# Second attention of a two-layer hybrid block: diagonal blocks from TensorE transposes, and the seam comparison in front of the last additions

## The chip, the cores and the metric

The kernel runs on one core of one Trainium2 chip. The metric is device time in microseconds of one execution. Everything is fp32. TensorE multiplies (a result lands in PSUM, in tiles of 128 partitions), ScalarE applies functions such as the exponential, VectorE and GpSimd do elementwise work, and queues move data between SBUF and HBM. The engines run side by side and wait for each other on semaphores.

## The reference

The input x has 8 images of 128 channels and 48 x 48 = 2304 positions. Two layers follow each other. The first is a causal attention over the positions, with a group norm in front. The second has two parts: a softmax attention without weights over layer-normed tokens, and then a batch-normed recurrence over layer-normed tokens.

```python
# layer 0
x = x + causal_attention(group_norm(x), Wq, bq, Wk, bk, Wv, bv)
# layer 1
t = to_tokens(x)                              # (8, 2304, 128)
h = layernorm(t)
attn = softmax(einsum('bnd,bmd->bnm', h, h))  # the second attention
t = t + einsum('bnm,bmd->bnd', attn, h)
# recurrence over the 2304 tokens
Wx = batchnorm(layernorm(t) @ W.T)
y_t = sigmoid(Wx_t + y_{t-1} @ V.T)
t = t + y
```

What matters here: in the second attention queries, keys and values are the same normed tokens h. The matrix of scores h h^T is symmetric, and so is its exponential. Each row is then divided by its own sum.

## The kernel before

**Blocks and chunks.** The 2304 tokens of an image are 18 blocks of 128 (`NB`), or 6 chunks of 384 (`NQ` chunks of `QC` columns, `QB` = 3 blocks each). For a chunk j of queries the second attention needs, for each block m of keys, p = exp(h_m h_j^T), a tile of 128 keys x 384 queries, and sums up h_m^T p in PSUM. The symmetry is already used between chunks: for blocks m behind the chunk (m's chunk over j) p is computed ("direct"), stored transposed through HBM, and read again as g when the other chunk comes ("turned"). Within a chunk's own 3 x 3 blocks it is not used: all three own tiles are computed in full.

**One step of the stream.** Each step has two halves. `begin` multiplies the scores and takes the exponential, with the row sums as a by-product. `product` multiplies p into the result, three steps later (`LAG = 3`). TensorE's stream is thus: score of step n, product of step n - 3, score of step n + 1, and so on; in "turned" steps only the product.

```python
class Full:
    def begin(self, j, what, first):
        b = self.b
        if first and j == 0:
            self.rows = small2.tile([P, NB, NQ], F32, tag="rows", name=f"rows_{b}")
        ...                                                     # cut: other chains, prefetch
        if what[0] == "turned":
            ...
            return self.loaded[i, j][:, :, g, :, :].rearrange("p a m r -> p m a r"), 0.0
        m = what[1]
        xh = x_hat[b][1]
        s = psum_s(f"s1_{b}_{j}_{m}")
        nc.tensor.matmul(s[:, :QC], xh[:, ts(m, P)], xh[:, ts(j, QC)], start=True, stop=True)   # L1212
        p = pp.tile([P, QC], F32, tag="p", name=f"p1_{b}_{j}_{m}")
        nc.scalar.activation(p, s[:, :QC], AF.Exp, bias=shift,
                             accum_out=self.rows[:, m, j : j + 1])                              # L1214
        return p, st.then(st.spend(QC * US), [("ACT", 0.58)])

    def product(self, j, what, o, p, ready, first, last):
        xhT = x_hat[self.b][0]
        if what[0] == "turned":
            ...
            nc.tensor.matmul(out_ap, xhT[:, QB * i + g, :], p, start=first, stop=last)          # L1222
        else:
            nc.tensor.matmul(o[:, :QC], xhT[:, what[1], :], p, start=first, stop=last)          # L1226
            if what[1] // QB > j:
                self.turned(j, what[1], p, ready)               # VectorE transposes p, to be stored
```

`st` is a bookkeeping of expected times that decides at build time where chains of smaller work are put into the stream; it issues nothing itself. `psum_s` has 4 buffers of one PSUM bank each, the pool of p has 6. The order of instructions is fixed by the program (`manual_schedule`). A chunk's own blocks come last in its list of direct steps, or first where j = 0. Chunk j = 0 shares its first steps with the end of the causal attention, and in the last chunk the steps of the next image's causal attention are interleaved.

**End of a chunk.** `after` turns the sums back to token-major order and adds the residual. `far` chooses between two ways for that, and is off in this attention (`FULL_FAR = False`). `sums` adds up `rows[:, 3j : 3j + 3, : j + 1]`.

**The recurrence.** The 2304 tokens are cut into 96 segments of 24 (`LS`), in three groups of 32 (`G`). All segments run side by side, each with a warm-up of 12 steps, so there are 36 steps for each group. In front of it stands a row of products whose result is not used (`idle`):

```python
idle(pw[:, 2 * P :], 14)                      # L1392: each an fp32 128x128 product
...
for t in range(-WARM, LS):
    for g in range(G):
        if s == 0 and t + TZ < LS:
            zs[g].append(inputs(g, t + TZ))   # VectorE, L1488: z = wx * a + c into PSUM
        nc.tensor.matmul(z[:, s], vT_f, prev[g], start=False, stop=True)    # L1539
        nc.scalar.activation(to, z[:, s], AF.Sigmoid)                       # L1541
        if s == TZ - 1:
            l0 = t + 1 - TZ
            if 0 <= l0 and (g or l0 >= LM):   # LM = 20
                if t < LS - 1:
                    add_residual(g, l0, y[g][:, so + 1 - TZ : so + 1])
            elif ...:                         # group 0 below LM: added by an accumulating DMA
        if t == LS - 1:
            seams(g)                          # last state of a segment against the next one's warm state

nc.vector.tensor_reduce(off, dm, AX.X, ALU.max)
nc.vector.tensor_scalar(off, off, STATE_TOL, None, ALU.is_gt)
for g in range(G):
    add_residual(g, LS - TZ, y[g][:, TO[g] - TZ :])
    if g:
        continue
    ...                                       # the flag: should the general path be run instead?
```

`add_residual` (L1521, L1522) adds on GpSimd for l0 < 20 and on VectorE for l0 = 20 and 22, and stores the result. Its VectorE buffers (`rlast`) are 3. `seams` is three VectorE operations for a group, two for the last (L1512 to L1515).

Of the kernel before, what the change touches and what calls it, by code (L numbers as in the profile page):

```python
# [14 lines left out]
F32 = mybir.dt.float32  # L15
AF = mybir.ActivationFunctionType
ALU = mybir.AluOpType
AX = mybir.AxisListType
# [586 lines left out]
def fast_path(ctx: ExitStack, tc: tile.TileContext, x, pe, w_ffn, out, x_tok, w_qkv, w_pos, v_t, gamma_beta, flag):  # L605
    nc = tc.nc
    B, C, H, W = x.shape
    N = H * W
    P = 128
    assert C == P and N % P == 0  # L610
    NB = N // P
    CH = 512
    QC = 384
    NQ = N // QC
    QB = QC // P
    SCALE = 1.0 / math.sqrt(P)
    US = 4 / 2400.0
# [7 lines left out]
    LS = N // SEGS  # L625
# [5 lines left out]
    LM = LS - 4  # L631
# [9 lines left out]
    ident = cpool.tile([P, P], F32, tag="ident", name="ident")  # L641
# [20 lines left out]
    with ExitStack() as actx:  # L662
# [11 lines left out]
        small2 = actx.enter_context(tc.tile_pool(name="small2", bufs=2))  # L674
# [4 lines left out]
        def psum_s(name):  # L679
            return ps_s.tile([P, CH], F32, tag="s", name=name)  # L680

        def psum_t(name):
            return ps_t.tile([P, CH], F32, tag="t", name=name)
# [43 lines left out]
        shift = apool.tile([P, 1], F32, tag="shift", name="shift")  # L727
# [45 lines left out]
        CAUSAL_FAR, FULL_FAR = True, False  # L773
        st = Stream()
# [341 lines left out]
        class Full:  # L1116
# [72 lines left out]
            def begin(self, j, what, first):  # L1189
                b = self.b  # L1190
                if first and j == 0:
                    self.rows = small2.tile([P, NB, NQ], F32, tag="rows", name=f"rows_{b}")
                if j == 0:
                    st.finish(normed_chunks[b, what[1] // QB])
                if first and b + 1 < B:
                    if j == 1:
                        norm_chain[b + 1] = st.add(group_norm(b + 1))
                    if j == NQ - 2:
                        st.finish(norm_chain[b + 1])
                        project(b + 1, 0)  # L1200
                self.prefetch()
                if what[0] == "turned":
                    i, g = what[1:]
                    while (i, j) not in self.loaded:
                        while self.pairs[len(self.loaded)] not in self.stored:
                            self.store()
                        self.load()
                    return self.loaded[i, j][:, :, g, :, :].rearrange("p a m r -> p m a r"), 0.0
                m = what[1]
                xh = x_hat[b][1]  # L1210
                s = psum_s(f"s1_{b}_{j}_{m}")
                nc.tensor.matmul(s[:, :QC], xh[:, ts(m, P)], xh[:, ts(j, QC)], start=True, stop=True)  # L1212
                p = pp.tile([P, QC], F32, tag="p", name=f"p1_{b}_{j}_{m}")
                nc.scalar.activation(p, s[:, :QC], AF.Exp, bias=shift, accum_out=self.rows[:, m, j : j + 1])  # L1214
                return p, st.then(st.spend(QC * US), [("ACT", 0.58)])

            def product(self, j, what, o, p, ready, first, last):
                xhT = x_hat[self.b][0]
# [13 lines left out]
            def after(self, j, o):  # L1232
                b, rows, tsum = self.b, self.rows, self.tsum
                cols = ts(j, QC)
                c = {}
                last = b == B - 1 and j >= NQ - 2
                far = FULL_FAR and not last
                if far:
                    ot = turn_result(o, f"f_{b}_{j}", c, True)
                    at = st.then(st.now, [("DVE", 0.57)])  # L1240
                    through = token_major(c, ot, f"f_{b}_{j}", "tof", 4)
                else:
                    o_sb = chunk_tile("o", f"of_{b}_{j}", c, 2)
                    nc.scalar.copy(o_sb, o[:, :QC])
                    at = st.then(st.now, [("ACT", 0.5)])
# [3 lines left out]
                def sums():  # L1249

                    dn = small2.tile([P, QB], F32, tag="dn", name=f"dn_{b}_{j}")
                    nc.vector.tensor_reduce(dn, rows[:, QB * j : QB * (j + 1), : j + 1], AX.X, ALU.add)
                    n = NQ - 1 - j
                    if n:
                        tp = psum_t(f"ts_{b}_{j}")
                        k = n * R * QB
                        nc.tensor.matmul(
                            tp[:, :k], same.rearrange("p a c -> p (a c)"), tsum[j][:, :n, :].rearrange("p n k -> p (n k)"),
                            start=True, stop=True,
                        )  # L1260
                        own = small2.tile([P, NQ - 1, R, QB], F32, tag="own", name=f"own_{b}_{j}")
                        nc.vector.tensor_mul(
                            own[:, :n].rearrange("p n a g -> p (n a g)"), tp[:, :k], mine[:, :n].rearrange("p n a g -> p (n a g)")
                        )
                        more = small2.tile([P, QB], F32, tag="more", name=f"more_{b}_{j}")
                        nc.vector.tensor_reduce(more, own[:, :n].rearrange("p n a g -> p g (n a)"), AX.X, ALU.add)
                        nc.vector.tensor_add(dn, dn, more)
                    ri = small.tile([P, QB], F32, tag="ri", name=f"ri_{b}_{j}")
                    nc.vector.reciprocal(ri, dn)
                    c["ri"] = ri  # L1270
# [100 lines left out]
                else:  # L1371
# [7 lines left out]
                c["chain"] = self.before["chain"] = st.add([  # L1379
                    *through,  # L1380
                    (sums, 0.15, [("DVE", 0.8)]),
                    (residual, 0.0 if far else 0.35, [("DVE", 3.2)]),
                    (rooted, 0.0, [("POOL", 0.9)]),
# [5 lines left out]
        def idle(tp, n):  # L1389

            for _ in range(n):
                nc.tensor.matmul(tp[:, :P], ident, ident, start=True, stop=True)  # L1392
# [26 lines left out]
        ready, o = {}, {}  # L1419
        for n in range(len(stream) + LAG):  # L1420
            if n < len(stream):
                part, j, what, first, last = stream[n]
                ready[n] = part.begin(j, what, first)
            if n >= LAG:
                part, j, what, first, last = stream[n - LAG]
# [12 lines left out]
    G = SEG_GROUPS  # L1438
    TZ = 2
    TO = [4] + [2] * (G - 1)  # L1440
    assert LS * SEGS == N and WARM % TZ == 0 and LS % TO[0] == 0 and SG * B * TZ == CH
    with ExitStack() as rctx:
        rc = rctx.enter_context(tc.tile_pool(name="rconst", bufs=1))
        rst = [rctx.enter_context(tc.tile_pool(name=f"rst{g}", bufs=4 if g == 0 else 6)) for g in range(G)]
        rres = rctx.enter_context(tc.tile_pool(name="rres", bufs=6))
        rlast = rctx.enter_context(tc.tile_pool(name="rlast", bufs=3))
        ps_z = [rctx.enter_context(tc.tile_pool(name=f"ps_z{g}", bufs=2, space=PSUM)) for g in range(G)]
        ps_w = rctx.enter_context(tc.tile_pool(name="ps_w", bufs=1, space=PSUM))

# [12 lines left out]
        pw = ps_w.tile([P, CH], F32, tag="w", name="pw")  # L1462
# [3 lines left out]
        for t in range(-WARM, -WARM + 2 * TZ, TZ):  # L1466
            for g in range(G):
                z = ps_z[g].tile([P, TZ, B, SG], F32, tag="z", name=f"z_{g}_{t}")
                nc.tensor.matmul(z.rearrange("p t b s -> p (t b s)"), zero[:, :P], zero, start=True, stop=True)
                banks[g].append(z)  # L1470
        idle(pw[:, 2 * P :], 14)

        mv = rc.tile([P, 2], F32, tag="bn_mv", name="bn_mv")
        nc.vector.bn_aggr(mv, stats)
# [23 lines left out]
        prev, warm, y = [], [], [None] * G  # L1498
# [10 lines left out]
        def seams(g):  # L1509
# [4 lines left out]
                nc.vector.tensor_sub(d[:, g, :, SG - 1 :], prev[g][:, :, SG - 1 :], warm[g + 1][:, :, 0:1])  # L1514
            nc.vector.tensor_reduce(dm[:, g : g + 1], d[:, g, :, :n], AX.XY, ALU.max, apply_absolute_value=True)  # L1515

        def add_residual(g, l0, yt):
            engine, pool = (nc.gpsimd, rres) if l0 < LM else (nc.vector, rlast)
            r = pool.tile([P, TZ, B, SG], F32, tag="r", name=f"r_{g}_{l0}")
            t2 = t2s[g].rearrange("p b (s l) -> p l b s", l=LS)[:, l0 : l0 + TZ] if g else t2l[:, l0 - LM : l0 - LM + TZ]  # L1520
            engine.tensor_add(r, yt, t2)  # L1521
            nc.sync.dma_start(out[g, :, l0 : l0 + TZ], r)  # L1522
# [7 lines left out]
        for t in range(-WARM, LS):  # L1530
            s = t % TZ
            for g in range(G):
                if s == 0 and t + TZ < LS:
                    zs[g].append(inputs(g, t + TZ))
                so = t % TO[g]
                if so == 0:
                    y[g] = rst[g].tile([P, TO[g], B, SG], F32, tag="y", name=f"y_{g}_{t}")
                z = zs[g][0]
                nc.tensor.matmul(z[:, s], vT_f, prev[g], start=False, stop=True, skip_group_check=True)  # L1539
                to = warm[g] if t == -1 else y[g][:, so]  # L1540
                nc.scalar.activation(to, z[:, s], AF.Sigmoid)  # L1541
                prev[g] = to
                if t == -1 and g == 0:
                    nc.vector.memset(warm[0][:, :, 0:1], 0.0)
                if s == TZ - 1:
                    zs[g].popleft()

                    l0 = t + 1 - TZ
                    if 0 <= l0 and (g or l0 >= LM):
                        if t < LS - 1:  # L1550
                            add_residual(g, l0, y[g][:, so + 1 - TZ : so + 1])
                    elif l0 >= 0 and so == TO[0] - 1:
                        nc.gpsimd.dma_start(out[0, :, t + 1 - TO[0] : t + 1], y[0], accum_op=ALU.add)
                if t == LS - 1:
                    seams(g)

        off = rc.tile([P, 1], F32, tag="off", name="off")
        nc.vector.tensor_reduce(off, dm, AX.X, ALU.max)
        nc.vector.tensor_scalar(off, off, STATE_TOL, None, ALU.is_gt)
        for g in range(G):  # L1560
            add_residual(g, LS - TZ, y[g][:, TO[g] - TZ :])
            if g:
                continue
            nc.tensor.matmul(pw[0:1, P : P + 1], off, ones[:, 0:1], start=True, stop=True)
            nc.vector.tensor_scalar(flag, pw[0:1, P : P + 1], fl[:, 1:2], 0.5, ALU.add, ALU.is_gt)
# [56 lines left out]
```

## Time and profile before

| What | Value |
|---|---|
| Time, median of 3 runs (lowest to highest) | 1782.08 us (1781.37 to 1783.71) |
| Span of the profiled execution | 1780.2 us |
| Mean granted TensorE clock | 0.991 |
| VectorE, ScalarE, GpSimd busy | 74%, 41%, 12% |
| Chain: scores of the second attention (L1212) | 18% |
| Chain: its direct products (L1226) | 18% |
| Chain: its turned products (L1222) | 12% |
| Chain: first attention, scores and products (L1011, L1022) | 17% and 17% |
| Chain: recurrence products (L1539) | 2% |

How to read it: the profile lists each instruction with its engine and line. A group's row gives the busy time, the mean duration of one, and the engine's idle time just before them with what ended it. The chain is followed back from the last instruction to what released it each time, so its shares say which engine's work sets the end. TensorE's products are pipelined: a record lasts longer than the step from one record to the next, and the step is what a product costs in a row. An fp32 product is two records, a transpose is one.

### The profile page before, as it was taken

How to read it: one execution, taken by the hardware profiler on the slowest of the kernel's cores; microseconds unless marked ns; L12 is line 12 of the kernel's file. 1: busy time of each engine (PE TensorE's matmuls, PEld its weight loads, DVE VectorE, ACT ScalarE, POOL GpSimd, SP SyncE). 2: the span in 40 equal slices, each digit the busy share in tenths (PEclk: the TensorE clock that was granted, in tenths of full speed). 3: DMA queues.
4: the chain of work that ended last, by engine and by line, in shares of the span. 5: the costliest groups of instructions: out<-in, count | busy, mean ns of one | idle time of the engine just before them, and what ended most of it. 6: DMA issues, size and time to landing. Idle time of an engine off the chain costs nothing.

```text
span 1780.2 us, 22179 instructions
## 1 busy us (share of the span) xinstructions
PE 1743.5 (98%) x6242; PEld 1093.8 (61%) x6243; DVE 1312.9 (74%) x3361; ACT 735.2 (41%) x1812; POOL 204.9 (12%) x305
## 2 busy tenths in 40 slices
PE   8999999999999999999999999999999999999995
PEld 5666566665666566665666656665666656665574
DVE  4868668866878668786688668786687866876477
ACT  2344424543345423443245433454234442454354
POOL 1110011000110001100110001100011001100026
PEclk8999999999999999999999999999999999999998
DMA  4405662257424584057722574235830576125857
GB/s 142 135 23 191 181 196 90 88 179 196 119 93 133 173 214 125 23 191 191 187 86 89 181 194 121 94 134 164 222 124 23 191 185 179 47 91 180 207 174 200
DMA packets 205576, 256.10 MB, mean 144 GB/s; under 512 B 89889, under 2 KB 175042, under 8 KB 205444
## 3 DMA queue, kind: packets, MB, share of 16 engines
q1 hardware_dynamic: 204492, 251.57, 48.3%
q0 software_dynamic: 720, 2.62, 1.0%
q8 instruction: 52, 0.85, 0.2%
q14 instruction: 80, 0.66, 0.1%
q10 hardware_dynamic: 232, 0.40, 0.1%
HBM read 150.24 MB, written 104.27 MB: 143 GB/s over the span
## 4 chain that ended last, share of the span: by engine, by line
PE 96%; DMA 1%; DVE 1%; issue 0%; ACT 0%; SPq 0%; POOL 0%; ACTq 0%; DVEq 0%; POOLq 0%
PE s L1212 18%; PE o L1226 18%; PE s L1011 17%; PE o L1022 17%; PE o L1222 12%; PE pj L872 4%; PE pj L875 2%; PE z L1539 2%; PE wx L1319 2%; PE tb L932 1%; PE of_t L932 1%; DVE r L1521 0%; PE pb L830 0%; DMA g<-e 0%; DMA x<-in_x_dram 0%
## 5 line engine op out<-in xcount | busy, mean ns | idle before, releaser
L1214 ACT ACTIVATE p<-s,shift 128x384 f32<-128x384 f32 x504 | 292.9, 581 | 486.8 <-PE s L1212 471.5
L1013 ACT ACTIVATE p<-s 128x384 f32<-128x384 f32 (+2 forms) x504 | 232.2, 461 | 440.3 <-PE s L1011 389.4
L1212 PE MATMUL s<-xh 128*128 128x384 f32 x1008 | 410.4, 489 | 0.0
L1226 PE MATMUL o<-p,xhT 128*128 128x384 f32 x1008 | 403.9, 487 | 4.4 <-ACT p L1214 4.4
L1011 PE MATMUL s<-q,k 128*128 128x384 f32 (+2 forms) x1008 | 382.4, 461 | 0.1
L1022 PE MATMUL o<-p,vT 128*128 128x384 f32 (+2 forms) x1008 | 377.8, 457 | 0.0
L1222 PE MATMUL o<-g,xhT 128*128 128x384 f32 x720 | 281.3, 488 | 0.8 <-DMA g<-e 0.8
L1226 PEld LDWEIGHTS o<-p,xhT 128*128 128x128 f32 x1008 | 189.0, 190 | 132.3 <-ACT p L1214 8.7
L1022 PEld LDWEIGHTS o<-p,vT 128*128 128x128 f32 x1008 | 189.0, 191 | 115.0 <-issue 1.1
L1212 PEld LDWEIGHTS s<-xh 128*128 128x128 f32 x1008 | 186.1, 190 | 115.0
L1011 PEld LDWEIGHTS s<-q,k 128*128 128x128 f32 x1008 | 182.8, 191 | 97.2 <-issue 0.6
L1037 DVE TENSOR_TENSOR acc<-acc,p 128x384 f32<-128x384 f32 (+2 forms) x408 | 209.0, 512 | 33.7 <-POOL p L1016 9.1
L1175 DVE STREAM_TRANSPOSE t<-p 128x384 f32<-128x384 f32 x360 | 187.3, 550 | 37.3 <-ACT p L1214 36.1
L1222 PEld LDWEIGHTS o<-g,xhT 128*128 128x128 f32 x720 | 133.2, 190 | 83.2 <-issue 2.2
L1183 DVE TENSOR_REDUCE tsum<-t 128x12 f32<-128x1152 f32 x120 | 162.4, 1353 | 4.2
L877 DVE TENSOR_TENSOR z<-pj,pb 128x384 f32<-128x384 f32 x144 | 78.9, 548 | 110.0 <-PE pj L872 92.0
L1016 POOL TENSOR_TENSOR p<-p,triu 128x128 f32<-128x128 f32 x144 | 72.8, 507 | 607.9 <-ACT p L1013 514.2
L1292 POOL TENSOR_TENSOR roots<-ve_f,mhalf 128x3 f32<-128x3 f32 x48 | 41.1, 856 | 521.0 <-DVE ve_f L916 521.0
L1214 ACT ACTIVATION_READ_ACCUMULATOR p<-s,shift 128x1 f32 x504 | 97.2, 193 | 0.0
L872 PE MATMUL pj<-xn,wT 128*128 128x384 f32 x192 | 79.8, 501 | 1.4 <-DVE xn L865 1.4
L922 POOL TENSOR_TENSOR rs_c<-ve_c,mhalf 128x3 f32<-128x3 f32 x48 | 45.2, 941 | 216.2 <-DVE ve_c L916 213.6
L1320 DVE TENSOR_TENSOR scale<-wx,scale 128x384 f32<-128x384 f32 x46 | 25.4, 552 | 56.3 <-PE wx L1319 56.3
(263 smaller groups left out, 1471.8 us busy)
## 6 DMA issues: line engine op xcount, KB each, us to landing
e<-t SPq DMA_DIRECT2D x120, 576.0 KB
g<-e SPq DMA_DIRECT2D x480, 144.0 KB
pb<-posb_d SPq DMA_DIRECT2D x46, 576.0 KB
t1t<-in_x_tok_dram SPq DMA_DIRECT2D x48, 192.0 KB
t_d<-tt SPq DMA_DIRECT2D x184, 48.0 KB
t2x<-t_d SPq DMA_DIRECT2D x46, 192.0 KB
scale<-rs SPq DMA_DIRECT2D x46, 192.0 KB
x<-in_x_dram SPq DMA_DIRECT2D x14, 576.0 KB
```

What stands on the lines that cost most here:

```text
L872: nc.tensor.matmul(ps[:, :QC], wT[:, j, :], xn, start=True, stop=True)
L877: nc.vector.tensor_add(z, ps[:, :QC], c["pb"][:, j, :])
L1011: nc.tensor.matmul(s[:, off:QC], keys[b][:, ts(m, P)], queries[b, j][:, off:], start=True, stop=True)
L1013: nc.scalar.activation(p[:, off:], s[:, off:QC], AF.Exp, scale=SCALE)
L1022: nc.tensor.matmul(o[:, off:QC], vals[b][:, ts(m, P)], p[:, off:], start=first, stop=last)
L1037: nc.vector.tensor_add(a[:, off:], a[:, off:], p[:, off:])
L1175: nc.vector.transpose(t[:, :, :, g, :].rearrange("p b j r -> p j b r"), p.rearrange("p (j b r) -> p j b r", j=QB, b=R))
L1183: nc.vector.tensor_reduce(self.tsum[j][:, n - j - 1, :], t.rearrange("p b j m r -> p (b j) (m r)"), AX.X, ALU.add)
L1212: nc.tensor.matmul(s[:, :QC], xh[:, ts(m, P)], xh[:, ts(j, QC)], start=True, stop=True)
L1214: nc.scalar.activation(p, s[:, :QC], AF.Exp, bias=shift, accum_out=self.rows[:, m, j : j + 1])
L1222: nc.tensor.matmul(out_ap, xhT[:, QB * i + g, :], p, start=first, stop=last)
L1226: nc.tensor.matmul(o[:, :QC], xhT[:, what[1], :], p, start=first, stop=last)
```

## The change

The change has two parts, and some smaller adjustments.

*First part.* Within a chunk's own 3 x 3 blocks of exp(scores), block (n, i) is the transpose of block (i, n). So for own block n only the columns from n on are multiplied and exponentiated. The i < n columns are taken from the older tiles of the same chunk by TensorE transposes, written into the free columns of the same score tile s, and copied from there into p by ScalarE, which sums their rows as well. This is meant to take work off TensorE: three blocks of scores in nine are replaced by three transposes. `rows` gets one more column for the copies' sums, set to zero beforehand.

*Second part.* At the end of the recurrence the additions for l0 = 20 are no longer made inside the loop. All six VectorE additions come after the loop, and so the seams are compared in front of them and the flag is known earlier. `rlast` gets a fourth buffer.

*Smaller ones.* The idle products in front of the recurrence go from 14 to 8. The condition in `far` is narrower (it stays off in either case).

```diff
                 if first and j == 0:
-                    self.rows = small2.tile([P, NB, NQ], F32, tag="rows", name=f"rows_{b}")
+                    self.rows = small2.tile([P, NB, NQ + 1], F32, tag="rows", name=f"rows_{b}")
+                    nc.gpsimd.memset(self.rows[:, :, 0:1], 0.0)
...
                 s = psum_s(f"s1_{b}_{j}_{m}")
-                nc.tensor.matmul(s[:, :QC], xh[:, ts(m, P)], xh[:, ts(j, QC)], start=True, stop=True)
+                n = m - QB * j if m // QB == j else 0
+                off = n * P
+                nc.tensor.matmul(s[:, off:QC], xh[:, ts(m, P)], xh[:, QC * j + off : QC * (j + 1)], start=True, stop=True)
                 p = pp.tile([P, QC], F32, tag="p", name=f"p1_{b}_{j}_{m}")
-                nc.scalar.activation(p, s[:, :QC], AF.Exp, bias=shift, accum_out=self.rows[:, m, j : j + 1])
-                return p, st.then(st.spend(QC * US), [("ACT", 0.58)])
+                nc.scalar.activation(p[:, off:], s[:, off:QC], AF.Exp, bias=shift, accum_out=self.rows[:, m, j + 1 : j + 2])
+                ready = st.then(st.spend((QC - off) * US), [("ACT", 0.36 + (QC - off) * 0.0006)])
+                if m // QB == j:
+                    if n == 0:
+                        self.own = []
+
+                    for i, (q, at) in enumerate(self.own):
+                        nc.tensor.transpose(s[:, ts(i, P)], q[:, ts(n, P)], ident)
+                        ready = st.spend(P * US / 2, at)
+                    if n:
+                        nc.scalar.activation(p[:, :off], s[:, :off], AF.Copy, accum_out=self.rows[:, m, 0:1])
+                        ready = st.then(ready, [("ACT", 0.36 + off * 0.0006)])
+                    self.own.append((p, ready))
+                return p, ready
...
-                far = FULL_FAR and not last
+                far = FULL_FAR and not (b == B - 1 and j >= NQ - 3)
...
-                    nc.vector.tensor_reduce(dn, rows[:, QB * j : QB * (j + 1), : j + 1], AX.X, ALU.add)
+                    nc.vector.tensor_reduce(dn, rows[:, QB * j : QB * (j + 1), : j + 2], AX.X, ALU.add)
...
-        rlast = rctx.enter_context(tc.tile_pool(name="rlast", bufs=3))
+        rlast = rctx.enter_context(tc.tile_pool(name="rlast", bufs=4))
...
-        idle(pw[:, 2 * P :], 14)
+        idle(pw[:, 2 * P :], 8)
...
+        ys = {}
+
         def add_residual(g, l0, yt):
...
                     l0 = t + 1 - TZ
+                    ys[g, l0] = y[g][:, so + 1 - TZ : so + 1]
                     if 0 <= l0 and (g or l0 >= LM):
-                        if t < LS - 1:
-                            add_residual(g, l0, y[g][:, so + 1 - TZ : so + 1])
+                        if l0 < LM:
+                            add_residual(g, l0, ys[g, l0])
...
-        for g in range(G):
-            add_residual(g, LS - TZ, y[g][:, TO[g] - TZ :])
-            if g:
+        for k, (l0, g) in enumerate((l, g) for l in range(LM, LS, TZ) for g in range(G)):
+            add_residual(g, l0, ys[g, l0])
+            if k:
                 continue
```

## The prediction

> **What bounds the kernel now.** I read the page first (busy shares, then the chain that ended last by engine), then the chain in order of time for what one step of TensorE costs, then the ScalarE groups by shape, and last the timeline of one wait and of the end.
>
> The page, busy time and chain:
> ```profile
> PE 1743.5 (98%) x6242; PEld 1093.8 (61%) x6243; DVE 1312.9 (74%) x3361; ACT 735.2 (41%) x1812; POOL 204.9 (12%) x305
> ...
> PE 96%; DMA 1%; DVE 1%; issue 0%; ACT 0%; SPq 0%; POOL 0%; ACTq 0%; DVEq 0%; POOLq 0%
> ```
> TensorE is busy for 98% of the span and carries 96% of the chain. So every microsecond taken from TensorE's stream comes off the time, and every microsecond in which TensorE is made to wait is added, while ScalarE (41%) has room to spare.
>
> The chain in order of time (start us, us, what), from a chunk of the second attention and from the start of the recurrence:
> ```profile
> 400.81 0.65 PE o L1222 x2
> 401.45 0.33 PE of_t L932 x3
> ...
> 405.01 0.66 PE s L1212 x2
> ...
> 406.21 0.68 ACT p L1214 x2
> 406.88 0.04 issue
> ...
> 1707.62 3.12 PE pw L1392 x28
> ...
> 1712.36 0.43 PE z_-12_14235 L1539 x2
> ```
> A product of 384 fp32 columns is two records and 0.645 us, one of 256 columns is 0.43, one of 128 columns is two records of 3.12 / 28 = 0.111, so 0.22. A 128x128 transpose is one record and 0.33 / 3 = 0.109. The ScalarE piece from 406.21 is one of the rare places where TensorE waited for an exponential.
>
> ScalarE groups by shape (busy us, mean ns, then its idle time before):
> ```profile
> L1214 ACT ACTIVATE p<-s,shift 128x384 f32<-128x384 f32 x504 | 292.9, 581 | 486.8 <-PE s L1212 471.5 <-PE o L1226 8.8 <-DVE st_c L913 6.4
> L1013 ACT ACTIVATE p<-s 128x384 f32<-128x384 f32 x408 | 200.4, 491 | 374.7 <-PE s L1011 343.0 <-DVE acc L1033 15.2 <-DVE acc L1037 11.3
> L1214 ACT ACTIVATION_READ_ACCUMULATOR p<-s,shift 128x1 f32 x504 | 97.2, 193 | 0.0
> ...
> L1013 ACT ACTIVATE p<-s 128x256 f32<-128x256 f32 x48 | 18.4, 384 | 42.5 <-PE s L1011 27.2 <-DVE acc L1037 15.2
> ...
> L1013 ACT ACTIVATE p<-s 128x128 f32<-128x128 f32 x48 | 13.3, 278 | 23.0 <-PE s L1011 19.1 <-DVE acc L1037 1.9 <-DVE mv_c L914 1.0
> ```
> The causal stage already uses all three widths: 491, 384 and 278 ns, 107 less for each block of 128 columns. The form with a row sum takes 581 and a separate read of the accumulator of 193.
>
> Timeline of that one wait (start us, us, engine, line, operation; idle time before it in brackets):
> ```profile
> 406.21 0.58 ACT L1214 ACTIVATE p<-s,shift 128x384 f32<-128x384 f32 x1
> ...
> 406.68 0.19 ACT L1214 ACTIVATION_READ_ACCUMULATOR p<-s,shift 128x1 f32 x1
> ...
> 406.93 0.59 PE L1226 MATMUL o<-p,xhT 128*128 128x384 f32 x1 [0.63 <-ACT p L1214]
> ```
> A waiting product starts only after the read of the accumulator has ended: 406.87 to 406.93. The exponential occupies 0.67 us from its start to the end of that read.
>
> Timeline of the end, VectorE:
> ```profile
> 1754.76 6.45 DVE L1521 TENSOR_TENSOR r<-y,t2l 128x512 f32<-128x512 f32 x1 [0.35 <-ACT y L1541]
> 1761.13 5.42 DVE L1521 TENSOR_TENSOR r<-y,t2s 128x512 f32<-128x512 f32 x2
> ...
> 1769.34 0.68 DVE L1521 TENSOR_TENSOR r<-y,t2l 128x512 f32<-128x512 f32 x1
> ```
> The same addition takes 0.68 us at 1769.34 and 6.45 at 1754.76, when GpSimd is adding too.
>
> **What the Trainium skill says.** PSUM — Partial Sum Buffer, section "PSUM bank collisions raise a hardware error": two engines may not be in the same bank and quadrant at once, even at disjoint columns, so guards have to go by bank and not by address. The trace of the kernel before cannot show it, since there each score tile has one writer and then one reader; but the built program of the changed kernel follows it (below), and my prediction rests on that. TensorE: Matmul & The Clock Gate, section "Part 4: PE-mode transpose", gives some 275 to 390 ns for a bf16 transpose; in this trace fp32 ones in a row are 109 ns apart, and I use that. SBUF — State Buffer, section "SBUF: two separate sides", says that VectorE with two SBUF inputs and GpSimd take turns at an exclusive lock; the 6.45 against 0.68 us agrees. ScalarE: Activation LUTs, section "Table sets: the hidden batching unit", has copy in every set; the trace has plain copies between exponentials and only two table loads in the whole run, so the new copies should load none.
>
> **The change part by part.** The second attention has 8 batches of 6 chunks, 48 in all. In each, three own blocks (n = 0, 1, 2) are touched.
>
> *Removed.* The score for n = 1 shrinks from 384 to 256 columns: 0.645 - 0.43 = 0.215. For n = 2 from 384 to 128: 0.645 - 0.22 = 0.425. Together 0.64 us a chunk.
>
> *Added on TensorE.* Three transposes at 0.109: 0.33 us. If nothing else happened, a chunk would gain 0.31 us and 48 chunks 15 us. That is what the change is for.
>
> *Added wait.* The transposes write into the very score tile s whose other columns the exponential of this same step is reading. In the built program the first transpose of n = 1 waits on ScalarE's semaphore for the exponential of its own tile (not for the older p that it transposes), and the first transpose of n = 2 likewise. TensorE's order there is score, transposes, product of three items earlier; nothing stands between score and transposes, so TensorE stands still for the whole round trip. For n = 1:
> - last score columns come out after the engine's slot: a record lasts 0.486 while the next starts 0.323 later, so 0.16;
> - score end to exponential start 0.04 (score at 400.32 + 0.49, exponential at 400.85);
> - exponential of 256 columns with its read: 0.67 - 0.107 = 0.56;
> - read end to TensorE 0.06 (406.87 to 406.93).
>
> That is 0.82 us. For n = 2 with 128 columns it is 0.107 less: 0.71. The first transpose after a wait is some 0.05 longer, because its weights could not be loaded ahead (324 ns for the waiting `tx` transposes against 273 for those in a row): 0.10 for two. Sum 1.63 us a chunk.
>
> *Net on TensorE.* 1.63 + 0.33 - 0.64 = +1.32 us a chunk, times 48 = +63 us.
>
> *ScalarE.* The exponentials get shorter, two copies with row sums are added (about 0.37 + 0.09 + 0.09 and 0.48 + 0.09, by the widths above). They lie off the path: the next product of that p is three items away. But now each exponential of n = 1 and 2 is on the path, so any other ScalarE work in front of it is too. The groups L1325, L1339, L1103 and L1244 are 52 + 18 + 23 + 23 = 116 us, over the 49% of the span (870 us) that the chain gives to this stage: a chance of 0.13 to meet one, with some 0.4 us left of it, for 96 exponentials: about +5 us.
>
> *Memset of one column of row sums, 8 times, on GpSimd:* off the path. *The other condition for `far`:* the flag in front of it is False, so nothing changes.
>
> *Idle products in front of the recurrence, 14 to 8.* Their 28 records end at 1710.74, while VectorE had the first group's inputs ready at 1709.07 (1708.76 + 0.30). Six fewer save 12 x 0.111 = 1.3 us, and the data is there by then: -1.3 us.
>
> *Seams in front of the additions.* VectorE has the same work after the last sigmoid: seams 2.9 us (1766.47 to 1769.43) and six additions. Only their order changes. Today VectorE is locked out from 1754.76 to about 1760.5 with an addition; afterwards it will be locked out with the seams' first subtraction, from some 1757.4 on. GpSimd's two last additions take their turn in between in both. I book 0, and the last store should start at about the same distance from the last sigmoid.
>
> Sum: 1782.1 + 63 + 5 - 1.3 = 1849 us.
>
> **The rivals.**
> 1. The transposes wait only for the older p, as the diff's own bookkeeping assumes, and that p is long there. Then the gain of 15 us is left, with 1.3 of the idle products: about 1766, within 2%. For it: the causal product between score and transpose gives ScalarE 0.65 us. Against it: the wait in the program names the exponential of the same tile, and TensorE takes its stream in order.
> 2. The wait is there but shorter, because the semaphore is raised by the exponential and not by its read, about 0.19 us less for each: 96 x 0.19 = 18 us, so about 1830. Against it: the product at 406.93 waited out the read.
> 3. ScalarE gets so far behind at some chunks that the waits grow: VectorE holds the p buffers in the first chunk of each batch. Twice my 5 us and a microsecond more in 16 places would give about 1870. Against it: in the kernel before, the exponentials of own blocks start right behind their scores almost everywhere.
> 4. The end: the seams get between GpSimd's additions sooner, or the six stores pile up in the queue; worth 2 us either way.
>
> **Range and chances.** The wait is a fact of the program and its terms are measured in this trace, so its size is the main uncertainty: 1.63 us give or take 0.25 a chunk is 12 us, the collisions 4, the end 2. Range 1833 to 1866. Faster by over 2% would need 1746 or less, over twice what the change could bring without any wait: 0.01. Within 2% needs rival 1, or a wait of half my size: 0.04. Slower by over 2% is the rest: 0.95.
>
> **What would show it.** In the profile after, TensorE's transposes of own blocks should be listed with idle time in front of them, released by ScalarE's exponential p, some 96 times and about 75 us in all, 0.7 to 0.9 us each; TensorE's share of the chain should fall by four points and ScalarE's rise by as much. The score line should have 96 records each of 256 and 128 columns at steps of 0.216 and 0.11, the transposes 0.109 to 0.17. The 16 idle records should end 1.3 us nearer to the first sigmoid. If those transposes show no idle time, or idle time that ends with another engine, or if TensorE's share stays at 98%, the prediction is wrong at its main step.

## The result, and the profile after

| | us, median | ratio to the kernel before (95% interval) |
|---|---|---|
| before | 1782.39 | |
| changed kernel | 1848.45 (1846.7 to 1849.59) | 1.0369 [1.0351, 1.0387] |

The changed kernel is 66 us slower, against 67 predicted.

The page of the changed kernel, busy time and chain:
```profile
PE 1748.7 (95%) x6375; PEld 1096.7 (59%) x6375; DVE 1311.3 (71%) x3361; ACT 760.3 (41%) x2004; POOL 205.8 (11%) x313
...
PE 89%; DVE 4%; ACT 3%; DMA 1%; issue 1%; SPq 1%; DVEq 0%; POOL 0%; ACTq 0%; POOLq 0%
```
TensorE's busy time has hardly changed (1743.5 before), but it is 95% of a longer span instead of 98%. The added time is idle time of the bounding engine. (Some 16 of the 1748.7 us are waiting too: the first 0.16 us of each of 96 waits counts as busy, as shown next.)

Who waited for whom, TensorE of the changed kernel (waiting line, what ended the wait; us in total, times, longest):
```profile
PE s L1225 <- ACT p L1218: 60.1, 95, 1.0
PE pw L1583 <- DVE off L1578: 8.0, 1, 8.0
PE o L1238 <- DMA g<-e: 4.2, 4, 1.5
```
The new first row is the transposes (L1225), which wait for the exponential (L1218) in nearly all of the 96 places. The row counts 60 us, since a product's record in this profile lasts until its last result and so covers the first 0.16 us of each wait. From the start of the last score record to the start of the transpose, less the step such a record costs in a row (0.216 and 0.109), the stops add up to 76.4 us.

One of them, in the timeline of the changed kernel (start us, us, then the instruction; in brackets its engine's idle time before it):
```profile
184.47 0.59 PE L1216 MATMUL s<-xh 128*128 128x256 f32 x2
...
185.10 0.47 ACT L1218 ACTIVATE p<-s,shift 128x256 f32<-128x256 f32 x1 [0.40 <-PE s L1216]
185.48 0.19 ACT L1218 ACTIVATION_READ_ACCUMULATOR p<-s,shift 128x1 f32 x1
...
185.72 0.33 PE L1225 MATMUL s<-ident,p 128*128 128x128 f32 x1 [0.66 <-ACT p L1218]
...
185.89 0.81 PE L1242 MATMUL o<-p,xhT 128*128 128x384 f32 x2
```
The score's two records would take TensorE until 184.90. The exponential starts at 185.10 and its read ends at 185.67, the transpose starts at 185.72: 0.82 us without work. The next product, which needs nothing from all this, stands behind the transpose in TensorE's queue and waits with it.

TensorE groups by shape in the changed kernel:
```profile
L1225 PE MATMUL s<-ident,p 128*128 128x128 f32 x144 | 36.8, 310 | 60.7 <-ACT p L1218 60.1 <-DMA g<-e 0.5
L1216 PE MATMUL s<-xh 128*128 128x256 f32 x96 | 28.6, 379 | 0.0
...
L1216 PE MATMUL s<-xh 128*128 128x128 f32 x96 | 18.5, 275 | 0.0
```
The cheaper scores and the transposes cost what the prediction says. Summed from start to start, the 96 changed scores, their stops and the 144 transposes take 128.9 us on TensorE, where 96 full scores at 0.645 took 61.9. The first part of the change thus costs 67.0 us by itself.

### The profile page after: what moved, and what is told of

Same layout as the page of the kernel before. It is cut to its first block, busy times and chain, and to the rows that moved or that the text cites. A ratio compares the mean times of both kernels' runs of the same rounds, so it can differ in the third digit from the quotient of the medians.

```text
span 1845.9 us, 22643 instructions
## 1 busy us (share of the span) xinstructions
PE 1748.7 (95%) x6375; PEld 1096.7 (59%) x6375; DVE 1311.3 (71%) x3361; ACT 760.3 (41%) x2004; POOL 205.8 (11%) x313
## 4 chain that ended last, share of the span: by engine, by line
PE 89%; DVE 4%; ACT 3%; DMA 1%; issue 1%; SPq 1%; DVEq 0%; POOL 0%; ACTq 0%; POOLq 0%
PE o L1242 17%; PE s L1216 16%; PE s L1011 15%; PE o L1022 15%; PE o L1238 12%; PE pj L872 3%; ACT p L1218 3%; PE s L1225 2%; PE z L1557 2%; PE wx L1335 2%; PE pj L875 1%; DMA g<-e 1%; PE tb L932 1%; PE of_t L932 1%; DVE z L877 1%
## 5 line engine op out<-in xcount | busy, mean ns | idle before, releaser
L1218 ACT ACTIVATE p<-s,shift 128x384 f32<-128x384 f32 (+2 forms) x504 | 277.5, 551 | 490.5 <-PE s L1216 485.6
L1216 PE MATMUL s<-xh 128*128 128x384 f32 (+2 forms) x1008 | 380.4, 459 | 1.7 <-ACT xh L1103 1.7
L1218 ACT ACTIVATION_READ_ACCUMULATOR p<-s,shift 128x1 f32 x504 | 97.2, 193 | 0.0
L1225 PE MATMUL s<-ident,p 128*128 128x128 f32 x144 | 36.8, 310 | 60.7 <-ACT p L1218 60.1
```

The costliest lines, as they stand in the source:

```text
L1216: nc.tensor.matmul(s[:, off:QC], xh[:, ts(m, P)], xh[:, QC * j + off : QC * (j + 1)], start=True, stop=True)
L1218: nc.scalar.activation(p[:, off:], s[:, off:QC], AF.Exp, bias=shift, accum_out=self.rows[:, m, j + 1 : j + 2])
```

## The experiments

The theory: the transposes have to wait for the exponential of their own step, because both use one PSUM bank, and TensorE has nothing else to do meanwhile since its queue is in order. (A score tile is one whole bank here, so no run tells a guard by bank from a guard by tile.) Rival A: they wait for the older p, or ScalarE is late in general. Rival B: narrow products and transposes cost more than their columns.

**A bank of its own for the transposes (run own_bank).**
```diff
+                    if n:
+                        tp = psum_t(f"own_{b}_{j}_{n}")
...
-                        nc.tensor.transpose(s[:, ts(i, P)], q[:, ts(n, P)], ident)
+                        nc.tensor.transpose(tp[:, ts(i, P)], q[:, ts(n, P)], ident)
...
-                        nc.scalar.activation(p[:, :off], s[:, :off], AF.Copy, ...)
+                        nc.scalar.activation(p[:, :off], tp[:, :off], AF.Copy, ...)
```


> The transposes of own blocks write into a PSUM tile of their own instead of the free columns of the score tile; everything else as in the changed kernel. Theory (TensorE waits because its transposes share a bank with the score that ScalarE is still reading, 1.53 us a chunk): the waits disappear, since the older p has been ready for long; 1848.5 - 76 - 5 (no restart of the first transpose) = about 1767 us, TensorE's idle time in front of the transposes under 5 us. Rival A (the wait is for the older p, or ScalarE is late in general): nothing changes, 1845 to 1850. Rival B (narrow products and transposes cost more than their columns): only part comes back, about 1810.

Measured: 1780.58 us, ratio 0.9989 [0.998, 0.9998] to the kernel before. The transposes in this run's list of one tile's instructions (count; shortest, median, longest in ns):
```profile
L1227 PE MATMUL own<-ident,p x144: 272/273/273, 121.4 to 1687.5; 128*128 128x128 f32 x144
```
All 144 have the length that they have in a row, none is lengthened by a wait, and in the list of waits they don't appear. So both rivals fall: nothing was changed but the tile, and with it the bank, that the transposes write and the copy reads. (The older p still has to be ready, and it is.) But the time is 14 us above the 1767 expected. Its list of waits, TensorE:
```profile
PE o L1240 <- DMA g<-e: 9.5, 7, 2.0
```
TensorE now waits for g in seven places, 1.4 us on average and 2.0 at most. In the changed kernel these waits were already 4.2 us, so the list explains only a part of the 14. The run own_pool takes this up.

**The transposes in front of the score, same bank (run turn_first).**
```diff
+                if n:
+                    for i, (q, at) in enumerate(self.own):
+                        nc.tensor.transpose(s[:, ts(i, P)], q[:, ts(n, P)], ident)
+                        ...                      # bookkeeping
                 nc.tensor.matmul(s[:, off:QC], xh[:, ts(m, P)], ...)
                 ...
-                    for i, (q, at) in enumerate(self.own):
-                        nc.tensor.transpose(s[:, ts(i, P)], q[:, ts(n, P)], ident)
-                        ...                      # bookkeeping
```


> Same bank as in the changed kernel, but the transposes stand in front of the score of their step, so that no exponential has read the tile yet; the transposes then wait only for the older p. Theory: the guard costs nothing in this order; what is left is the older p where only one product (0.645 us) lies between: 0.93 - 0.645 = 0.28 for n = 1 in the first chunk of an image, 0.82 - 0.645 = 0.17 for n = 2 in the first two or three; some 7 us in all, so about 1775 us. Rival A (the older p): about 1845, as the distance to the older p gets shorter, not longer. Rival B: about 1810.

Measured: 1773.50 us, 0.9955 [0.9938, 0.9972], below the kernel before. The same instructions in the same bank, in another order, are 75 us faster than in the changed kernel. Two kinds of stop are left. In 16 of the 96 places the transpose of n = 1 waits 0.28 us, 4.5 us in all, the size expected for an older p with one product in between. One of them:
```profile
118.94 0.81 PE L1022 MATMUL o<-p,vT 128*128 128x384 f32 x2
119.86 0.33 PE L1218 MATMUL s<-ident,p 128*128 128x128 f32 x1
```
The two records of the product take TensorE until 118.94 + 0.645 = 119.58, and the transpose starts at 119.86. In 16 other places the second transpose of n = 2 waits, the one that reads the p of n = 1, for 0.07 us each, 1.1 us in all. Here 0.17 was expected; the first transpose of that step (0.109) also stands in between, which the expectation left out. The run also settles rival A from the other side: here the transposes stand nearer to the older p and wait less.

**The transposes one product later (run turn_late).**
```diff
+                    def turn():
+                        ...                      # the same transposes and copy
+                    if n:
+                        late.append(turn)
 ...
                 part.product(j, what, o[part, j], *ready.pop(n - LAG), first, last)
+                while late:
+                    late.popleft()()
```


> Same bank, same wait for the exponential of the same tile, but transposes and copy stand one product (0.645 us) later in TensorE's stream. Theory: of each wait 0.645 us is filled with work, 0.82 - 0.645 = 0.17 and 0.71 - 0.645 = 0.07 are left, 12 us over 48 chunks and some 3 for ScalarE's other work: about 1785 us. Rival A: the older p is one step older here, so no wait at all, about 1767. Rival B: about 1810.

Measured: 1796.05 us, 1.0076 [1.0059, 1.0092]. The waits shrink as the theory says: from 76.4 us to 15.3 in all 96 places, where 12 + 3 was expected. So 0.645 us of work in between removes just about that much of each wait. The total is 11 us over the 1785 expected. The waits for g are 7.5 us, 3.3 more than in the changed kernel; where the rest is I did not trace.

**Without the row sum (run no_sum).** The exponentials of own blocks 1 and 2 leave out their row sums.
```diff
...                                              # the preset of the row sums
+                if n:
+                    nc.scalar.activation(p[:, off:], s[:, off:QC], AF.Exp, bias=shift)
+                else:
                     nc.scalar.activation(..., bias=shift, accum_out=self.rows[:, m, j + 1 : j + 2])
```


> As the changed kernel, but the exponentials of own blocks 1 and 2 leave out their row sums (the sums are preset with a constant, so the output is not the reference's). Theory: the wait ends with the read of the accumulator, so each of the 96 waits is shorter by 0.56 - 0.38 = 0.18 us: 1848.5 - 17 = about 1831 us. Rival (the semaphore is raised by the exponential itself): at most the 0.09 by which the form with a sum is longer, about 1840.

Measured: 1841.07 us, 1.0331 [1.0314, 1.0349]. The waits fall by 8.7 us, 0.09 each, half of what I expected. The timeline of one of them:
```profile
186.40 0.47 ACT L1219 ACTIVATE p<-s,shift 128x256 f32<-128x256 f32 x1 [0.41 <-PE s L1216]
...
186.93 0.33 PE L1228 MATMUL s<-ident,p 128*128 128x128 f32 x1 [0.57 <-ACT p L1219]
```
The release still comes 0.05 us after ScalarE's last record of the step (186.87 to 186.93), now that of the exponential. The time is close to the rival's 1840, but not for the rival's reason: if the exponential itself released the transpose, both kernels would show the same step from its end, and that step is 0.15 us in the changed kernel (185.57 to 185.72) and 0.06 here. What was wrong is the length without a sum: I had put in the causal stage's 384 ns, and it is 0.47, just as long as with the sum. The groups by shape say why. The first row is the changed kernel's exponential with the sum, the second its copy with a sum:
```profile
L1218 ACT ACTIVATE p<-s,shift 128x256 f32<-128x256 f32 x48 | 22.8, 474 | 71.5 <-PE s L1216 71.5
...
L1228 ACT ACTIVATE p<-s 128x256 f32<-128x256 f32 x48 | 18.4, 384 | 25.3 <-PE s L1225 25.3
```
Both have a sum and differ by 90 ns; the exponential takes a per-partition bias tile (`shift`), as it does in no_sum, the copy and the causal exponential do not. So in these forms the 90 ns go with the bias and not with the sum; no run takes the bias out of one and the same exponential. The sum costs the wait the separate read, of which 0.10 us stick out.

**The end alone (run end_only).** The changed kernel with the second attention of before.

> The changes at the end alone (8 idle products, additions after the seams, fourth buffer), with the second attention as before. Theory: -1.3 us from the idle products (seen between the end of the batch statistics and the first sigmoid, 5.1 to 3.8 us) and -1.9 from the last sigmoid to the end (22.0 to 20.1 us), as in the changed kernel: 1782.5 - 3.2 = about 1779 us. The prediction's 0 for the seams would give 1781.

Measured: 1780.03 us, 0.9984 [0.9976, 0.9993]. From the end of the batch statistics to the first sigmoid it is 3.8 us (5.1 before), from the last sigmoid to the end 20.3 (22.0 before). Both gains are there; their sum of 3.0 us lies within the interval (1.2 to 4.3 us).

**The flag last (run flag_last).**
```diff
-            if k:
+            if k < 5:
                 continue
```


> As the run with the end alone, but the flag is worked out behind the last of the six additions instead of behind the first. Theory (the gain of 1.9 us behind the last sigmoid comes from the flag being known early, so that TensorE's long branch of 3.7 us is over before the last store): the gain is lost, 22 us or more from the last sigmoid to the end, about 1781 us or more. Rival (it comes from the order of additions and seams on VectorE): the gain stays, 20 us, about 1779 us.

Measured: 1782.41 us, 0.9999 [0.9991, 1.0008]. From the last sigmoid to the end it is 22.9 us, against 20.3 in end_only. So the gain at the end goes with the place of the flag and not with the order of additions and seams. The last store and TensorE's conditional branch on the flag, first in flag_last, then in end_only:
```profile
1771.70 0.33 SPq L1524 DMA_DIRECT2D out_dram<-r  x1
L1582 PEldq COMPARE_BRANCH  x1: 3757/3757/3757, 1772.4 to 1772.4; - x1
```
```profile
1773.79 0.59 SPq L1524 DMA_DIRECT2D out_dram<-r  x1
L1582 PEldq COMPARE_BRANCH  x1: 3397/3397/3397, 1768.4 to 1768.4; - x1
```
The last store is issued 14.2 and 14.3 us behind the last sigmoid, so the 2.6 us lie behind the stores: 8.7 us to the end against 6.0. The branch lasts 3.4 to 3.8 us on TensorE in these traces, on the other engines 0.05 to 0.07. It ends 4.2 us before the end in flag_last, 8.0 in end_only and 5.7 in the kernel before. That the branch is what holds up the end is thus a guess, since this distance is not the same in flag_last and in the kernel before; it was not tried by itself.

**The small stores on GpSimd's queue (runs own_pool and first_pool).** In own_bank's first image the loads of g for the last chunk stand in the queue behind seven small stores, which are issued from 226.1 to 230.7 us.
```diff
-                        nc.sync.dma_start(d[g], roots_t[j % 2][g :: SQ])
+                        nc.gpsimd.dma_start(d[g], roots_t[j % 2][g :: SQ])
...
-                        nc.sync.dma_start(d[r], c["tt"][ts(r, SQ)]...)
+                        nc.gpsimd.dma_start(d[r], c["tt"][ts(r, SQ)]...)
```


> As the run with a bank of its own for the transposes, but the seven small stores at a chunk's end (roots and turned tokens) are issued from GpSimd's queue instead of the queue that also loads g. Theory (the bank run fell 13 us short of 1767 because without the waits TensorE reaches the last chunk's g before the loads, which stand in the queue behind those stores): TensorE's waits for g fall from 9.5 us to under 4, about 1773 us. Rival (the loads are late for another reason, the transfers themselves or the buffers of g): the waits stay, 1780 us.

Measured for own_pool: 1771.70 us, 0.9939 [0.9924, 0.9954]. The waits for g are gone from the list, as the theory says, and a new one has come:
```profile
PE o L1022 <- POOL p L1016: 8.8, 6, 1.8
```
The causal masks of the next image are made on GpSimd, and stood behind the stores of chunk 4 there. The new waits are about as long as the old ones (8.8 and 9.5 us) and the time still fell by 8.9 us, so the two lists don't account for all of it.

> The same move of the seven small stores, on the run with the transposes in front of the score. Waits for g are only 2.2 us there, so at most 2 us are to be had: about 1772 us. If issuing on GpSimd delays the chains (its roots, its locked port), it gets slower, 1776 or more.

Measured for first_pool: 1779.73 us, 0.9978 [0.9967, 0.9988], slower than turn_first. It got waits for the masks too (6.4 us) and had only 2.2 us of waits for g to lose.

**Both waits avoided (runs own_mix and end_mix).**
```diff
                 def spread():
+                    queue = nc.gpsimd if j < 4 else nc.sync
...                                              # the seven stores: queue.dma_start
```


> Transposes in a bank of their own; the seven small stores go through GpSimd's queue for chunks 0 to 3 only, and stay in the loading queue for chunks 4 and 5, whose stores fall among the next image's masks on GpSimd. Theory: neither the waits for g (9.5 us in the bank run) nor those for GpSimd's masks (8.8 us with all stores moved) are there, so 1771.7 - 8 = about 1764 us, with TensorE's share of the chain back at 95% or more. If the masks were late for another reason, about 1771.

Measured for own_mix: 1765.26 us (1764.43 to 1766.19), 0.9898 [0.9882, 0.9915]. Its page, with the chain, and the head of TensorE's waits:
```profile
PE 1729.7 (98%) x6375; PEld 1100.6 (62%) x6375; DVE 1312.1 (74%) x3361; ACT 748.8 (42%) x2004; POOL 333.5 (19%) x537
...
PE 92%; DVE 4%; DMA 2%; issue 1%; POOL 0%; ACT 0%; SPq 0%; DVEq 0%; POOLq 0%; ACTq 0%
```
```profile
PE pw L1586 <- DVE off L1581: 8.0, 1, 8.0
PE pj L872 <- DVE xn L865: 2.5, 2, 1.4
```
No wait of more than 2.5 us in all is left but the one at the end, which costs nothing to TensorE's work. TensorE is busy for 98% again, with 14 us less to do than before. Its share of the chain was expected at 95% and is 92%.

> Control: the same split of the small stores, with the second attention as before and the changes at the end. TensorE hardly waits for g there (0.8 us in the kernel before), so moving the stores should bring nothing: 1780 us as for the end alone. If it brings 5 us or more, the gain of the run before is not due to the transposes' freed time but to the queue alone.

Measured for end_mix: 1780.05 us, 0.9985 [0.9976, 0.9994], the same as end_only. So the queue alone brings nothing; it only stops taking away what the transposes bring. In own_mix and end_mix it is 21.6 us from the last sigmoid to the end instead of 20.3 in end_only; GpSimd's closing DRAIN lasts 8.9 us there, 0.5 in end_only, and ends 0.8 us before the end. The fastest version is own_mix, 18 us under the kernel before beside it (1783.72).

## Why the prediction was right

*The saved and added work of TensorE.* Right in each term. In own_mix the 96 changed scores take 31.4 us from start to start and the 144 transposes 15.7, where 96 full scores took 61.9: 14.8 us less. Own_mix is also 14.8 us faster than end_mix, which lacks only the transposes. So the 15 us the change is for are real.

*The wait and its cause.* Right. The steps 0.16, 0.04, 0.56 and 0.06 are found one by one at 184.47 to 185.72, as 0.16, 0.04, 0.57 and 0.05. Moving the transposes to another bank removed it, moving them in front of the score left 5.5 of the 76.4 us, and putting one product in between removed one product's worth. With the shortest stop of each kind in all places, 0.819 and 0.715 us, they would be 73.6 in all, against 73.4 predicted; the rest to 76.4 is 2.8 us, where I had 5 for ScalarE's other work. One reading was wrong without harm: the 90 ns between 581 and 491 were put down to the row sum, and go with the bias (no_sum). So the copies take 278 and 384 ns, not 0.09 us more; they are off the path.

*The longer first transpose.* 144 transposes take 21.1 us from start to start instead of 15.7: 0.06 for each of 96, against 0.05.

*What the profile would show.* I said some 75 us of idle time in front of the transposes; the list says 60.1, because I had forgotten there that the profile's own ends cover 0.16 us of each. I had expected TensorE's share of the chain to go to ScalarE. It fell from 96 to 89%, but ScalarE took only 3 and VectorE 4. VectorE has the same 4% in own_mix, where the waits are gone, so this share is not a good measure of the wait.

*Idle products.* From the batch statistics to the first sigmoid it is 5.12 us before and 3.78 after, -1.3 as predicted. The sign I gave for it does not hold: the idle records end 0.8 us before the first sigmoid in both kernels.

*Seams.* I booked 0 and it was -1.9 us. The step that failed is "VectorE has the same work, only its order changes": true, but it overlooked that the flag is also known earlier. The last store starts 14.3 us behind the last sigmoid, 14.7 before, about as predicted; most of the gain lies behind it. The lockout itself came as described, here in VectorE's timeline of the changed kernel:
```profile
1824.99 3.56 DVE L1528 TENSOR_TENSOR d<-y,warm 128x248 f32<-128x248 f32 x1 [2.94 <-ACT y L1559]
...
1832.12 0.41 DVE L1528 TENSOR_TENSOR d<-y,warm 128x248 f32<-128x248 f32 x1
```
The same subtraction takes 3.56 us beside GpSimd's additions and 0.41 after them.

*The rivals.* The first (only the older p) is what the reordered run turn_first makes true. The second put 0.19 us on the read of the accumulator; it is 0.10. The third, ScalarE far behind, did not happen: the longest stop is 1.16 us. The fourth gave the end 2 us either way; the size is right, but it came with the place of the flag, which that rival did not name.

*The total.* That 66 us stand against 67 is in part luck. The first part cost 67.0 us where 63 + 5 = 68 was booked, the 1.9 us at the end were not booked, and neither was the growth of TensorE's other waits, leaving out the one at the very end, from 14.1 to 16.0 us, in which the waits for g rise from 0.8 to 4.2. The last two cancel.

## What to carry to other kernels

Before filling the free columns of a PSUM tile from TensorE while another engine reads the rest, look in the built program for what the write waits on: in this program the guard covers the whole tile, which is one bank, so the "free" columns cost a full round trip through the other engine, 0.82 us here. Write first and let the reader come after, or take another bank. And on an engine that bounds the kernel, price a dependency by what stands between the two instructions in its queue, not by whether the engine at the other end is idle. When such a stop is removed, look again at the transfers, since what they were hidden behind is then gone (waits for g: 4.2 us in the changed kernel, 9.5 in own_bank).

## What was not expected of the hardware

- A ScalarE exponential with a per-partition bias tile takes 90 ns more here than one without (474 and 384 ns at 256 columns), and it does so without the row sum too (473 ns in no_sum). The sum itself shows only in the separate read.
- TensorE's conditional branch on a loaded flag lasts 3.4 to 3.8 us in the four traces read for it, where ScalarE, VectorE and GpSimd take 0.05 to 0.07.
- Seven small stores in GpSimd's queue occupy it for 0.55 to 0.63 us each, 4.0 us in a row (own_pool, 239.24 to 243.25), which was enough to make masks late that TensorE needs.
